# Expert products and channel moments on ScalarE, finer dealt preparation, and a spread ahead of the last stores, in a four-layer kernel

## The chip, the core and the metric

The kernel runs on one core of a Trainium2 chip. Its time is the device time of one execution in microseconds (us), and lower is better. A core has five engines that each execute their own instructions in order: TensorE (PE, with its weight loads shown as PEld), VectorE (DVE), ScalarE (ACT), GpSimd (POOL) and SyncE (SP, which in this kernel issues nearly all DMA transfers). They meet through semaphores. Tiles live in pools: a tile may be written only when those who used its place before are done.

## The reference, cut to what matters

Three images of 256 channels and 48 x 48 pixels go through four layers, each of the form x + layer(groupnorm(x)):

```python
x = x + conv1x1/attention block(_gn(x))          # layer 0
x = x + _L1_conv_ref(_gn(x), routing_ws, weight) # layer 1
x = x + _L2_conv_ref(_gn(x), weight, bias)       # layer 2
x = x + _L3_conv_ref(_gn(x), ...)                # layer 3, a scan over pixels

# layer 1: a 3x3 kernel of its own for each image
routing = sigmoid(pooled @ routing_ws)
ws = einsum('ne,eoihw->noihw', routing, weight)  # 8 experts
# layer 2: a 3x3 convolution with bias
# layer 3: (z, u projected; dt = softplus(...); causal conv of 4 taps)
hst = hst * exp(dt * A) + dt * B * u             # 512 rows x 16 states
y   = sum_n(hst * C) + u * D;  out = (y * silu(z)) @ out_proj
```

`_gn` is a group norm over 32 groups of 8 channels. Everything is float32.

## The kernel before, in words

An image is held in on-chip memory as `xs[b]`, 128 partitions x 2 channel halves x 2304 pixels. The images are handled in the order 2, 1, 0. Three parts follow one another.

**Layer 0** (to about 1600 us) has its order of instructions written out and pinned. Beside its end the kernel for image 2 of layer 1 is mixed.

**The conv stage** (about 1600 to 2140 us) does layers 1 and 2: six *units* (layer, image), two halves of an image each. Its order on each engine is chosen by a scheduler from the order of the program. A 3x3 convolution is done as six products per output block: `input_transform` pads and scales a half (ACT, L304, into `xpad`, of which there is one buffer), and twelve DVE instructions (L318 to L329) make `vt` of it (two buffers). `products` does six matmuls per product (L1331), `output` copies one of a pair (ACT, L1346, tile `cb`) and combines them on DVE (L1348 to L1361). Each half has two outputs of 128 channels; there are 144 matmuls in a unit. The product buffers in PSUM are five.

The kernels that are multiplied are made beside the units before. `mixed(b)` loads 48 pieces of 128 x 768, multiplies each by its image's routing weight and adds it up on DVE: L271 for expert 0, L273 for the other seven. `kernel_transform` (L254 to L259) follows. `plain` loads layer 2's kernel through a staging tile, copies it (L284) and transforms it. Unit 0 has `mixed(1)` beside it, unit 1 `mixed(0)`, unit 2 `plain`; each call of `next(beside...)` gives one step, 13 after each output. The transformed kernels `u` lie in two pools in turn.

Group norms of layers 2 and 3 are computed by `group_norm`: per image twelve `bn_stats` (DVE, L176) and two aggregations (L179), two small matmuls across the group (`ps_gm`, `ps_gv`), a few small DVE instructions, and a power on POOL (L162). The norm of layer 2 is called with the next unit's transform, that of layer 3 at the end of a unit of layer 2, where the image is also stored to memory (`xd`, L1401, six transfers on SP) so that the scan can fetch it in chunks.

From unit 4 on, `between()` in `output` deals one step of `early_preparation` at a time, four times in each output. These steps prepare chunk 0 of the scan and part of chunk 1: `group_scale` (ACT, L1043, with the image's norm), `less_mean` (PE, L1053), `centre`, `square_mean` (PE, L1060), `inverse_root`, `normalise`, `taps` (PE, L1095), `project_u` (L1115), `project_dt` (L1141), `softplus`. What is left is run when the units are done.

**The scan** (about 2140 us to the end) does layer 3 in 18 chunks of 384 pixels (6 per image), 8 steps each (four blocks of 128 rows, two halves of the states), order pinned again. `spread` fetches dt and dt*u of a block back from memory so that rows lie as the scan wants them: eight DMAs on SP, `dtr` (192 KB) and `dtur` (96 KB) in turn (L1444). In a step DVE fills half of a tile `hs` (L1474) and POOL the other half (L1478), ACT computes eight decays (L1503), DVE does eight scans (L1511; the first four on DVE's half, the last four on POOL's), POOL multiplies by C (`times_c`, L1519), and PE adds the states up (L1536). The program runs, ahead of step 0:

```python
k.rows = {0: spread(k, 0)}; spread_pe(k, 0); first_states(0); fill(0)
for n in range(3):
    decay(n)
for _, _, _, stage in gating:
    stage(k)
```

`gating` is the list of `project_z` (PE, L1172) and `take_z` (ACT, L1180) of a chunk; for later chunks these are dealt into the steps by `run`, with a last two of `take_z` in the list `after`.

Of the kernel before, what the change touches and what calls it, by code (L numbers as in the profile page):

```python
# [9 lines left out]
F32 = mybir.dt.float32  # L10
# [6 lines left out]
P = 128  # L17
B = 3
HW = 48
# [64 lines left out]
def net(  # L84
# [79 lines left out]

    def norm_steps(views, mat, psum, tag, stats=None):

# [3 lines left out]
        n = len(views)  # L170
        mv = small.tile([P, 2, 2], F32, name="mv")
        for i, view in enumerate(views):
# [32 lines left out]

    def group_norm_steps(b, psum, tag, stats=None):

        mv, gm, rstd = yield from norm_steps(
            [xs[b][:, ct, :] for ct in range(CT)], gmat, psum, tag, stats
        )  # L210
# [50 lines left out]
    def mixed(b, pool):  # L261

        u = weights[b] = pool.tile([P, 6, 3, CT, 256], F32, name="u")
        for e in range(EXPERTS):
            for ct in range(CT):
                for dx in range(3):
# [3 lines left out]
                    if e == 0:  # L270
                        nc.vector.tensor_scalar(dst, wt, re, None, ALU.mult)  # L271
                    else:
# [921 lines left out]
    def store(k, mo):  # L1194
# [63 lines left out]
    def early_preparation():  # L1258
# [4 lines left out]
        k = chunks[0]  # L1263
        yield
        group_scale(k)
        yield
# [27 lines left out]
        silu(k.u)  # L1294
        yield

        while 1 not in norm3:
            yield
# [6 lines left out]
        for m in (0, 2):  # L1305
# [7 lines left out]
            yield  # L1313
        k = chunks[1]
        for stage in (group_scale, less_mean, centre, square_mean, inverse_root, normalise):
            stage(k)
            yield
        tokens(k)


    with ExitStack() as l1:
# [5 lines left out]
        def products(u, vt, m, i):  # L1327
            pc = ps.tile([P, 512], F32, tag="c", name="ps_c")
            for ct in range(CT):
                for dy in range(3):  # L1330
# [3 lines left out]
                        start=ct == 0 and dy == 0, stop=ct == CT - 1 and dy == 2,  # L1334
                    )
            return pc[:, :HN]

        def output(b, h, m, u, vt, bias):
# [4 lines left out]
            for i, j in ((1, 3), (4, 5)):  # L1343
# [7 lines left out]
                sums += [add, sub]  # L1351
                between()
            p, q, r, s = sums
# [6 lines left out]
            for i, k, f in ((0, 0, 1.5), (2, 3, 6.0)):  # L1360
                stt(xj[:, k], products(u, vt, m, i), f, xj[:, k], ALU.mult, ALU.add)  # L1361
                between()

# [3 lines left out]
        halves = [(k, h) for k in range(len(units)) for h in range(2)]  # L1367

        def transformed(n):
            k, h = halves[n]  # L1370
            layer, b = units[k]
            if layer and h == 0:
                _, sc, sh = group_norm(b, pss, "s")
                norms[b] = sixth(sc, sh)
            return input_transform(b, h, *norms[b])
# [8 lines left out]
        vt = first_v  # L1384
        for n, (k, h) in enumerate(halves):
            layer, b = units[k]
# [11 lines left out]
            if layer and h == 1:  # L1398
                phases = xs[b].rearrange("p t (j n) -> p (t j) n", j=4)
                for c in range(NCH):  # L1400
                    nc.sync.dma_start(  # L1401
                        xd[b][:, c].rearrange("p t (j n) -> p (t j) n", j=4),
                        phases[:, :, c * (CH // 4) : (c + 1) * (CH // 4)],
                    )
                _, sc, sh = group_norm(b, pss, "s")
                keep = const.tile([P, 2, CT], F32, name=f"norm3{b}")
                nc.vector.tensor_copy(keep[:, 0, :], sc)
                nc.vector.tensor_copy(keep[:, 1, :], sh)
                norm3[b] = keep[:, 0, :], keep[:, 1, :]
        for _ in early:  # L1410
# [8 lines left out]
    with ExitStack() as l3:  # L1419
        wp = l3.enter_context(tc.tile_pool(name="w3", bufs=1))  # L1420
        psd = l3.enter_context(tc.tile_pool(name="psd", bufs=1, space=PSUM))
        psr = l3.enter_context(tc.tile_pool(name="psr", bufs=1, space=PSUM))
        psy = l3.enter_context(tc.tile_pool(name="psy", bufs=1, space=PSUM))

        scn = l3.enter_context(tc.tile_pool(name="scn", bufs=2))
        for name in ("u", "dtu", "bc0", "bc1", "sz"):
# [9 lines left out]
        def spread(k, m):  # L1436

            dtr = scn.tile([P, 4, CH], F32, name="dtr")
            dtur = scn.tile([P, 2, CH], F32, name="dtur")
            for i in range(4):  # L1440
                r = slice(32 * i, 32 * i + 32)
                for t, src in ((dtr, k.dtd), (dtur, k.dtud)):
                    src = src[m & 2][:, m & 1, :]
                    nc.sync.dma_start(t[r], src.rearrange("(q d) n -> d q n", d=32))  # L1444
# [267 lines left out]
```

## Time and profile before

| what | value |
|---|---|
| median of 3 runs | 3651.91 us |
| lowest, highest | 3649.39, 3655.53 us |
| the profiled execution | 3652.18 us, span 3650.2 us, granted clock 0.928 |
| busy PE, DVE, ACT, POOL | 3195.5, 3058.1, 2272.8, 1440.6 us |
| layer 0, conv stage, scan | about 1600, 540 and 1510 us |

The page and the views give times from the start of the span. A timeline row is: start, length (both us), engine, line, operation, out<-in with shapes, count, and in square brackets the idle time ahead of it and what ended that. A windows row is: start:end and length, then the busy time and number of instructions of PE, PEld, DVE, ACT and POOL, the granted clock of PE (1.00 is full), the mean busy share of the 16 DMA engines, and GB/s. One matmul of 128 x 128 by 128 x 288 shows as two records.

### The profile page before, as it was taken

How to read it: one execution, taken by the hardware profiler on the slowest of the kernel's cores; microseconds unless marked ns; L12 is line 12 of the kernel's file. 1: busy time of each engine (PE TensorE's matmuls, PEld its weight loads, DVE VectorE, ACT ScalarE, POOL GpSimd, SP SyncE). 2: the span in 40 equal slices, each digit the busy share in tenths (PEclk: the TensorE clock that was granted, in tenths of full speed). 3: DMA queues.
4: the chain of work that ended last, by engine and by line, in shares of the span. 5: the costliest groups of instructions: out<-in, count | busy, mean ns of one | idle time of the engine just before them, and what ended most of it. 6: DMA issues, size and time to landing. Idle time of an engine off the chain costs nothing. (4 is left out here: it accounts for less than half of the span.)

```text
span 3650.2 us, 45624 instructions
## 1 busy us (share of the span) xinstructions
PE 3195.5 (88%) x17154; PEld 1440.2 (39%) x17154; DVE 3058.1 (84%) x3398; ACT 2272.8 (62%) x3408; POOL 1440.6 (39%) x386
## 2 busy tenths in 40 slices
PE   6999999999999998877799987878888888878885
PEld 4323232342322324445577753333333333333331
DVE  3798989859889895479987559999999999999997
ACT  2688787748878874220012237777777777777774
POOL 0000000000000000210000039999999999999998
PEclk9999999999999999888899988988888999988887
DMA  4000000000000002645502223444444434443441
GB/s 172 10 1 1 1 2 1 1 39 1 1 1 1 1 1 79 209 140 208 203 19 65 51 72 99 102 117 103 114 108 105 107 97 110 101 119 99 115 105 36
DMA packets 167672, 266.50 MB, mean 73 GB/s; under 512 B 42689, under 2 KB 133633, under 8 KB 165266
## 3 DMA queue, kind: packets, MB, share of 16 engines
q1 hardware_dynamic: 155346, 245.80, 24.1%
q10 hardware_dynamic: 12096, 17.70, 1.5%
q8 instruction: 136, 2.23, 0.3%
q14 instruction: 94, 0.77, 0.1%
HBM read 216.31 MB, written 46.89 MB: 72 GB/s over the span
## 5 line engine op out<-in xcount | busy, mean ns | idle before, releaser
L597 ACT ACTIVATE pt<-ps_s 128x1024 f32<-128x1024 f32 x972 | 938.9, 1022 | 237.6 <-PE ps_s L593 220.2
L1511 DVE TENSOR_TENSOR_SCAN hs<-ps_da,hs 128x385 f32<-128x385 f32 x1152 | 1012.7, 939 | 71.9 <-ACT ps_da L1503 56.6
L673 DVE TENSOR_TENSOR part<-part,pt 128x2048 f32<-128x2048 f32 x396 | 906.5, 2289 | 78.5 <-ACT pt L597 53.9
L1503 ACT ACTIVATE ps_da<-dtr,u 128x384 f32<-128x384 f32 x1152 | 657.8, 582 | 314.6 <-DVE hs L1511 289.0
L162 POOL TENSOR_TENSOR rstd<-ve,mhalf 128x2 f32<-128x2 f32 (+1 forms) x26 | 17.3, 668 | 1683.1 <-DVE ve L160 1683.1
L593 PE MATMUL ps_s<-q,kt 32*128 32x512 f32 (+1 forms) x4320 | 616.8, 595 | 2.3 <-DVE q L554 0.9
L606 PE MATMUL acc<-pt,vt 128*32 128x512 f32 (+1 forms) x4320 | 523.7, 563 | 8.1 <-DVE o L653 8.0
L1331 PE MATMUL ps_c<-vt,u 128*128 128x288 f32 x1728 | 432.4, 412 | 65.4 <-DVE u L259 39.6
L1519 POOL TENSOR_TENSOR hc<-hs,x 128x3072 f32<-128x3072 f32 x72 | 444.4, 6172 | 48.6 <-PE ps_g L1141 15.6
L1519 POOL TENSOR_TENSOR hc<-hs,bc 128x3072 f32<-128x3072 f32 x72 | 444.0, 6167 | 36.2 <-PE ps_g L1141 13.6
L1331 PEld LDWEIGHTS ps_c<-vt,u 128*128 128x128 f32 x1728 | 331.4, 193 | 160.9 <-issue 67.3
L1095 PE MATMUL ps_g<-u 128*128 128x384 f32 x1152 | 385.9, 490 | 0.0
L593 PEld LDWEIGHTS ps_s<-q,kt 32*128 32x128 f32 x4320 | 219.9, 183 | 390.1 <-issue 230.2
L1095 PEld LDWEIGHTS ps_g<-u 128*128 128x128 f32 x1152 | 213.9, 189 | 170.2 <-issue 11.2
L1536 PE MATMUL ps_y<-hc,u 128*32 128x384 f32 x2304 | 244.1, 547 | 27.2 <-POOL hc L1519 23.9
L1478 POOL TENSOR_TENSOR hs<-dtur,x 128x1536 f32<-128x1536 f32 x72 | 247.8, 3442 | 19.4 <-DMA dtr<-dtd 11.5
L1478 POOL TENSOR_TENSOR hs<-dtur,bc 128x1536 f32<-128x1536 f32 x72 | 248.2, 3447 | 8.1 <-ACT ps_g L1073 4.9
L606 PEld LDWEIGHTS acc<-pt,vt 128*32 128x32 f32 x4320 | 95.7, 108 | 364.6 <-issue 329.0
L1346 ACT COPY cb<-ps_c 128x288 f32<-128x288 f32 x48 | 19.1, 398 | 297.6 <-PE ps_c L1331 248.8
L1141 PE MATMUL ps_g<-wconv,u 17*128 17x384 f32 x144 | 79.2, 684 | 97.2 <-ACT x L1162 97.2
L1172 PE MATMUL ps_g<-u 128*128 128x384 f32 x288 | 112.7, 526 | 39.1 <-ACT x L1180 23.3
L1053 PE MATMUL ps_g<-wconv,u 128*128 128x384 f32 x144 | 87.9, 784 | 67.3 <-ACT x L1162 67.3
(231 smaller groups left out, 3486.2 us busy)
## 6 DMA issues: line engine op xcount, KB each, us to landing
wconv<-in_we SPq DMA_DIRECT2D x144, 384.0 KB, 4.4
dtr<-dtd SPq DMA_DIRECT2D x288, 192.0 KB, 3.7
dtur<-dtud SPq DMA_DIRECT2D x288, 96.0 KB, 3.2
wconv<-xd SPq DMA_DIRECT2D x36, 384.0 KB, 4.4
x<-bcd SPq DMA_DIRECT2D x72, 192.0 KB, 5.7
dtd<-x SPq DMA_DIRECT2D x36, 384.0 KB, 2.4
bc<-bcd SPq DMA_DIRECT2D x72, 192.0 KB, 5.2
yc<-ycat ACTq DMA_DIRECT2D x18, 576.0 KB, 5.6
```

The costliest lines, as they stand in the source:

```text
L593: nc.tensor.matmul(s[:, j, cols], kt[r, mt * P : (mt + 1) * P], q[r, :n], start=True, stop=True,)
L597: nc.scalar.activation(p[:, h0 : h0 + 2, :], s, AF.Exp)
L606: nc.tensor.matmul(acc[h * HD : (h + 1) * HD, :n], vt[:, mt, g * P + h * HD : g * P + (h + 1) * HD], p[:, h, cols], start=mt == 0, stop=mt ...
L673: nc.vector.tensor_tensor(part, first_p if group == 1 else part, p, ALU.add)
L1095: nc.tensor.matmul(bank[m % 2], w3v["wtap"][:, tap, ct, m * P : (m + 1) * P], k.xn[:, ct, tap : tap + CH], start=tap == 0 and ct == 0, sto ...
L1172: nc.tensor.matmul(bank[j], w("in", ct * 512 + m * P, P), k.xn[:, ct, DCONV - 1 :], start=ct == 0, stop=ct == CT - 1,)
L1331: nc.tensor.matmul(pc[:, :HN], u[:, i, dy, ct, m * P : (m + 1) * P], vt[:, i, ct, dy * TW : dy * TW + HN], start=ct == 0 and dy == 0, stop ...
L1478: nc.gpsimd.tensor_tensor(hs[:, :, 2:4, 1:], k.rows[m][1].unsqueeze(1).broadcast_to([P, 2, 2, CH]), bb, ALU.mult,)
L1503: nc.scalar.activation(slots[n % 3][:, 1 : CH + 1], chunks[at].rows[m][0][:, q, :], AF.Exp, scale=amat[:, col : col + 1],)
L1511: nc.vector.tensor_tensor_scan(b, slots[(8 * s + part) % 3][:, : CH + 1], b, 0.0, ALU.mult, ALU.add)
L1519: nc.gpsimd.tensor_tensor(hc, tiles[s][:, :, :, 1:], cb.broadcast_to([P, 2, 4, CH]), ALU.mult)
L1536: nc.tensor.matmul(k.y_ps[32 * q : 32 * q + 32, :CH], fold, hc[:, g, q, :], start=False, stop=h == 1 and g == 1,)
```

## The change

1. `mixed`: the product of expert 0 is done by ACT (an activation Copy with the routing weight as its scale) rather than by DVE.
2. `plain`: layer 2's kernel is loaded straight into `u`, without staging tile and copy.
3. The norms of layers 2 and 3, all but the last image's, take their channel mean and variance from `moments`: on ACT, two passes per channel half over 2304 pixels, whose element output goes to a buffer of `xpad` that nobody reads. The rest of a norm (`next_norm`) is dealt out by `between()`.
4. `between()` is called after each product, six times in each output. The early preparation waits for the norm of image 2, the steps for chunk 1 come ahead of the wait for the norm of image 1, and `project_z` and `take_z` of chunk 0 are its last steps; the scan's start no longer runs `gating`, and the two `take_z` in `after` are left out for chunk 0.
5. The last image's stores to `xd` are issued by ACT's queue rather than SP's. The scan's two pools are given `reuse_waits="tile"`: a tile in them waits for those who used its own place, not for all of the pools that lay there. `spread` issues all four `dtr` ahead of the four `dtur`.

```diff
     def mixed(b, pool):
...
                     if e == 0:
-                        nc.vector.tensor_scalar(dst, wt, re, None, ALU.mult)
+                        nc.scalar.activation(dst, wt, AF.Copy, scale=re)
...
     def plain(pool):
...
-                wt = part_of_kernel(w2, ct, dx)
-                nc.vector.tensor_copy(u[:, dx, :, ct, :], wt)
+                nc.sync.dma_start(
+                    u[:, dx, :, ct, :],
+                    w2[ct * P : (ct + 1) * P, dx * 768 : (dx + 1) * 768].rearrange(
+                        "p (y o) -> p y o", y=3
+                    ),
+                )
...
-        (0, MID, 0, lambda k: take_z(k, 2, 0)),
-        (0, MID, 0, lambda k: take_z(k, 3, 1)),
+        (0, MID, 0, lambda k: k.at and take_z(k, 2, 0)),
+        (0, MID, 0, lambda k: k.at and take_z(k, 3, 1)),
...
     def early_preparation():
...
+        while 2 not in norm3:
+            yield
         group_scale(k)
...
+        k = chunks[1]
+        for stage in (group_scale, less_mean, centre, square_mean, inverse_root, normalise):
+            stage(k)
+            yield
+        tokens(k)
+        yield
+
+        k = chunks[0]
         while 1 not in norm3:
             yield
...
-        k = chunks[1]
-        for stage in (group_scale, less_mean, centre, square_mean, inverse_root, normalise):
-            stage(k)
+        for m in (0, 2):
+            for j in range(2):
+                project_z(k, m + j, j)
             yield
-        tokens(k)
+            for j in range(2):
+                take_z(k, m + j, j)
+            yield
...
         def products(u, vt, m, i):
...
+            between()
             return pc[:, :HN]
...
+        def moments(b):
+
+            mv = small.tile([P, 2, 2], F32, name="mv")
+            less = small.tile([P, CT], F32, name="lessm")
+            waste = pad.tile([P, 4, CT * (HR + 2) * PW + 2], F32, name="xpad")
+            waste = waste.rearrange("p j n -> p (j n)")[:, :N]
+            for ct in range(CT):
+                nc.scalar.activation(
+                    waste, xs[b][:, ct, :], AF.Identity, scale=1.0 / N,
+                    accum_out=mv[:, ct, 0:1],
+                )
+                nc.scalar.activation(
+                    less[:, ct : ct + 1], mv[:, ct, 0:1], AF.Identity, scale=-1.0 / HW
+                )
+                nc.scalar.activation(
+                    waste, xs[b][:, ct, :], AF.Square, bias=less[:, ct : ct + 1],
+                    scale=1.0 / HW, accum_out=mv[:, ct, 1:2],
+                )
+            return mv
+
+        def next_norm(layer, b):
+
+            last = layer and b == ORDER[-1]
+            known = None if last else moments(b)
+            for _ in range(5):
+                yield
+            _, sc, sh = yield from group_norm_steps(b, pss, "s", known=known)
...
         def between():
+            next(pending, None)
             if at_unit >= 4:
                 next(early, None)
...
+                queue = nc.sync if k + 1 < len(units) else nc.scalar
                 for c in range(NCH):
-                    nc.sync.dma_start(
+                    queue.dma_start(
...
+            if h == 1:
+                for _ in pending:
+                    pass
+                pending = next_norm(layer, b)
+                next(pending)
...
-        wp = l3.enter_context(tc.tile_pool(name="w3", bufs=1))
+        wp = l3.enter_context(tc.tile_pool(name="w3", bufs=1, reuse_waits="tile"))
...
-        scn = l3.enter_context(tc.tile_pool(name="scn", bufs=2))
+        scn = l3.enter_context(tc.tile_pool(name="scn", bufs=2, reuse_waits="tile"))
...
-            for i in range(4):
-                r = slice(32 * i, 32 * i + 32)
-                for t, src in ((dtr, k.dtd), (dtur, k.dtud)):
-                    src = src[m & 2][:, m & 1, :]
+            for t, src in ((dtr, k.dtd), (dtur, k.dtud)):
+                src = src[m & 2][:, m & 1, :]
+                for i in range(4):
+                    r = slice(32 * i, 32 * i + 32)
                     nc.sync.dma_start(t[r], src.rearrange("(q d) n -> d q n", d=32))
...
         for n in range(3):
             decay(n)
-        for _, _, _, stage in gating:
-            stage(k)
-
```

More of the change, by code (lines that the diff above doesn't have):

```diff
@@ L163, in rsqrt_eps, with norm_steps @@
         return r[:, :n]
-    def norm_steps(views, mat, psum, tag, stats=None):
+    def norm_steps(views, mat, psum, tag, stats=None, known=None):
         n = len(views)
-        mv = small.tile([P, 2, 2], F32, name="mv")
-        for i, view in enumerate(views):
+        mv = known
+        if known is None:
+            mv = small.tile([P, 2, 2], F32, name="mv")
+        for i, view in enumerate(views if known is None else ()):
             if stats is None:
@@ L204, in norm_stats, with group_norm_steps @@
         return at_once(norm_steps(*args))
-    def group_norm_steps(b, psum, tag, stats=None):
+    def group_norm_steps(b, psum, tag, stats=None, known=None):
         mv, gm, rstd = yield from norm_steps(
-            [xs[b][:, ct, :] for ct in range(CT)], gmat, psum, tag, stats
+            [xs[b][:, ct, :] for ct in range(CT)], gmat, psum, tag, stats, known
         )
@@ L1351, in output @@
                 sums += [add, sub]
-                between()
             p, q, r, s = sums
@@ L1361, in output @@
                 stt(xj[:, k], products(u, vt, m, i), f, xj[:, k], ALU.mult, ALU.add)
-                between()
         units = [(layer, b) for layer in range(2) for b in ORDER]
@@ L1367, in net @@
         halves = [(k, h) for k in range(len(units)) for h in range(2)]
+        def moments(b):
+            mv = small.tile([P, 2, 2], F32, name="mv")
+            less = small.tile([P, CT], F32, name="lessm")
[20 more added lines that the diff above has]
+            _, sc, sh = yield from group_norm_steps(b, pss, "s", known=known)
+            if layer == 0:
+                norms[b] = sixth(sc, sh)
+            else:
+                keep = const.tile([P, 2, CT], F32, name=f"norm3{b}")
+                nc.vector.tensor_copy(keep[:, 0, :], sc)
+                nc.vector.tensor_copy(keep[:, 1, :], sh)
+                norm3[b] = keep[:, 0, :], keep[:, 1, :]
         def transformed(n):
             k, h = halves[n]
[L1371 to L1375, printed above, removed]
+            return input_transform(units[k][1], h, *norms[units[k][1]])
         early = early_preparation()
@@ L1384, in net @@
         vt = first_v
+        pending = iter(())
         for n, (k, h) in enumerate(halves):
@@ L1404, in net @@
                     )
[L1405 to L1409, printed above, removed]
+            if h == 1:
[3 more added lines that the diff above has]
+                next(pending)
+        for _ in pending:
+            pass
         for _ in early:
```

## The prediction

> **What bounds the kernel now.** I read the rows in forty slices first, then windows over the conv stage, its waits, and the timeline around the seam to the scan. PE is full until slice 16, less so in slices 17 to 20, full again, and from slice 24 on POOL is. The change touches only the stretch from about 1600 us (first conv unit) to about 2180 us (second scan step). Windows over it (start:end, length, busy time and count of PE, PEld, DVE, ACT, POOL, granted clock, DMA share, GB/s):
>
> ```profile
> 1645.00:1700.00 55.00, 54.11 (x223) 41.76 (x221) 54.31 (x80) 5.07 (x8) 0.69 (x3) 1.00 0.68 236
> 1700.00:1725.00 25.00, 0.12 (x1) 0.15 (x1) 24.66 (x37) 0.00 (x0) 0.00 (x0) 0.60 0.57 206
> 1725.00:1797.00 72.00, 71.98 (x288) 55.76 (x288) 71.03 (x109) 8.33 (x12) 1.40 (x6) 0.97 0.62 210
> 1797.00:1819.00 22.00, 0.25 (x1) 0.28 (x2) 22.00 (x33) 0.00 (x0) 0.00 (x0) 0.58 0.45 155
> 1890.00:1966.00 76.00, 76.00 (x317) 59.67 (x316) 51.14 (x118) 8.69 (x13) 2.19 (x8) 1.00 0.13 39
> 2044.00:2139.00 95.00, 95.00 (x383) 71.30 (x381) 48.38 (x116) 21.80 (x34) 1.18 (x1) 1.00 0.25 63
> ```
>
> DVE is full up to 1819 while PE has two holes; afterwards PE is full and DVE half idle. So up to 1818.75, where PE starts unit 2, a microsecond off DVE is a microsecond; from there to the last conv matmul at 2139.24 (called E) only PE's work and stalls count. PE's timeline names what ended the holes:
>
> ```profile
> 1724.88 72.11 PE L1331 MATMUL ps_c<-vt,u 128*128 128x288 f32 x288 [24.98 <-issue]
> 1818.75 11.60 PE L1331 MATMUL ps_c<-vt,u 128*128 128x288 f32 x35 [21.77 <-DVE u L259]
> ```
>
> The second waits for DVE's last kernel transform, and so by DVE's full row does the first. Between 1818.75 and E PE waits once, 1.17 us at 1861.34 for a norm (mv L179). The products that the change moves:
>
> ```profile
> 1645.48 1.93 DVE L271 TENSOR_SCALAR u<-wconv,route 128x768 f32<-128x768 f32 x2
> 1647.68 3.77 DVE L271 TENSOR_SCALAR u<-wconv,route 128x768 f32<-128x768 f32 x4
> 1737.16 3.76 DVE L271 TENSOR_SCALAR u<-wconv,route 128x768 f32<-128x768 f32 x4
> 1743.42 1.92 DVE L271 TENSOR_SCALAR u<-wconv,route 128x768 f32<-128x768 f32 x2
> ```
>
> Both groups of six lie in the DVE-bound part; L176 (norm statistics, 35.8 us in this stage, all after 1833 us) and L284 (copies, from 1831 us) lie in the PE-bound one. The seam:
>
> ```profile
> 2140.09 2.83 SPq L1401 DMA_DIRECT2D xd<-x  x3
> 2147.53 1.76 DVE L1474 TENSOR_TENSOR hs<-ps_r,x 128x1536 f32<-128x1536 f32 x1 [2.99 <-DMA xd<-x]
> 2147.62 0.32 SPq L1444 DMA_DIRECT2D dtr<-dtd  x1
> 2154.90 1.59 ACT L1503 ACTIVATE ps_da<-dtr,u 128x384 f32<-128x384 f32 x3 [7.02 <-DMA dtr<-dtd]
> 2155.57 6.81 POOL L1478 TENSOR_TENSOR hs<-dtur,x 128x1536 f32<-128x1536 f32 x2 [11.51 <-DMA dtr<-dtd]
> 2160.92 1.81 DVE L1511 TENSOR_TENSOR_SCAN hs<-ps_da,hs 128x385 f32<-128x385 f32 x2 [2.74 <-ACT ps_da L1503]
> 2163.42 0.48 ACT L1180 COPY x<-ps_g 128x384 f32<-128x384 f32 x1 [2.03 <-PE ps_g L1172]
> 2166.97 2.66 DVE L1511 TENSOR_TENSOR_SCAN hs<-ps_da,hs 128x385 f32<-128x385 f32 x3 [4.25 <-ACT ps_da L1503]
> ```
>
> Here nothing is full: the spread (dtr, dtur) starts only when the last stores of x have landed, then the scans wait for decays (L1503), which stand behind take_z (L1180) on ACT, which waits for projections on PE. Step 0 ends at 2169.55, E + 30.3. Later POOL does 3.44 + 6.17 = 9.6 us in a pace of about 10.3 per step.
>
> **Part 1, first expert product on ACT.** Removed from DVE's full part: twice six at a pace of 0.93 us (3.76 for four), 11.2 us. The six for image 2 lie beside attention, where DVE isn't the limit: nothing. Two costs. The sixth product of unit 0 stands behind the wait for a staging buffer and before the second copy of a product (cb, L1346); the DMA that supplies L273 cost 2.0 us of waits in all before, and I take 0.7 more (0 to 3). And unit 1 now holds nine small instructions of unit 0's norm (rows of 0.13 to 0.17 us, 0.07 to 0.1 apart) that ran after 1860 before: 0.8. Net -9.7, range -7 to -12. The Trainium skill ("ScalarE: Activation LUTs", Rules for kernel authors) speaks against the move: multiplication belongs on VectorE. Its cost section on the same page makes one product 186 + 93 + 0.833 x 768 = 919 ns, an estimate. The rows: a 128x768 ACTIVATE took 844 ns (L1068), L271 took 1003 ns, and ACT was busy 5.07 of 55 us. If ACT were the limit, the rule would make this part nought; being idle it gives the 11.2. I go by the rows.
>
> **Part 2, copies and norms.** Kernel 2 is loaded straight into u: six copies less on DVE, 6 x 0.94 = 5.6 us. Five of six norms go to ACT: sixty L176 at 0.47 pace, 28 us. All that is cover removed from an engine that was half idle beside a full PE: 0, except that the 1.17 us stall goes. Had PE not been the limit there, it would be worth up to 34 us. The kernel's six loads wait for unit 1's last matmul; I place them about 20 us ahead of the first use. ACT gets, per unit, two Identity and two Square of 128x2304. From 128x768 (0.844) and 128x1536 (1.483), 0.833 us per 1000 elements, one takes an estimated 2.1 us, so 9 us per unit. They write to the padding buffer, of which there is one: the next unit's padding (L304) and transform wait. Counted from a unit's start S: norms to S+5, padding to S+8, twelve transform instructions at 0.72 to S+17; PE needs the result at S+35. Slack some 18 us: 0.
>
> **Part 3, finer dealing, and gates.** Preparation is dealt after each of six products per output instead of four times, and projections of z for chunk 0 (eight matmuls, 16 records of 0.34 at L1172) come into the full PE: +5.5. In the order of instructions as built, less_mean of chunk 0 stands 57 matmuls into unit 4, and now waits for group_scale on ACT, which waits for the norm of that image. Norm ready at S+27.7, two L1043 to S+30; PE is there at S+28: 2.0, and square_mean right behind it 0.6. Stage: -1.2 + 5.5 + 2.6 = +6.9, range +4 (no stall) to +12 (three more such stalls). No record of before shows this dealing.
>
> **Part 4, the seam.** Stores of the last image go to ACT's queue; the pools of the scan are released tile by tile, so the first dtr waits for E and not for the landing at about E+8; all dtr are issued ahead of dtur; take_z has left the start. Decays: four dtr issued E to E+1.9, landing 4.1 later by the row, E+6. DVE's first fill waits only for the norm chain, E+5.3 to E+7.1, so scans begin near E+7 (before E+16.3). POOL needs dtur. By the waits as built, the second to fourth dtur reuse the completion semaphores of the three last stores, so they are issued only when those have landed: stores issued by ACT at E+0.9 to E+2.8, landing 5.5 to 6.2 after issue, E+8.4; dtur lands 3.2 to 3.7 after that, E+12; POOL's 3.44 ends at E+15.5. DVE does four scans of its own half to E+10.6, waits, and four of POOL's at 0.9 by E+19.4. Before E+30.3, so -10.9. Of this the old stalls, 2.74 + 4.25 = 7.0, are take_z's. Range -8 to -15.3 (semaphores don't bind; then scans run without pause to about E+15). A new table load (1.28 us) is done before decay data arrive. The skill's page "DMA: Bandwidth & Descriptors" (Issuing engines are not separate DMA queues) says that another issuing engine saves only issue time: by that the store's move is worth at most 2.8 us, the row's issue time. The row of dtr at 2147.62 shows a wait for landing, 4.5 us past the last issue, and that wait is removed by the pools' release, not by the queue; so the rule bounds one edit, and I keep 10.9.
>
> **Part 5, steady scan.** Same instructions in the same order on PE, DVE, ACT and POOL. Within a spread dtr comes first, the last dtur is still eighth. 0, but 0.1 us per spread over 72 would be 7 us, so I allow 5 either way.
>
> **Sum.** -9.7 + 6.9 - 10.9 = -13.7 on the profiled run of 3652.18 (span 3650.2 and 2.0 around it), 0.3 above the median 3651.91: 3638.5, about -0.37 %. This kernel's measurement can tell about 0.2 % from no change, 7.3 us.
>
> **Rivals.** (a) The semaphores of the stores don't hold up dtur, and the dealing makes no stall: -9.7 + 4.3 - 15.3 = -20.7, 3631. For: dtur waits are for single transfers, which may land sooner with less traffic. Against: the waits are in the program. Chance 0.2. (b) Gains are given back: two or three more dealing stalls (+5), 7 instead of 9.7 and 8 instead of 10.9: -3.1, 3649, within 0.2 %. For: DVE and ACT execute in order, and one late preparation step delays the copies and sums that free PE's product buffers. Against: units 4 and 5 had no stall before at a coarser dealing. Chance 0.12. (c) Slower: the hand-overs PE to ACT to DVE to PE in units 4 and 5. With six dealings per output they are one product apart, 12 records of 0.243, 2.9 us, not 4.4. A step that takes copy 0.48, table loads of 1.28 and two ACTIVATEs of 0.84 is longer than 2.9, and PE then stands still. Some twelve hand-overs; the sum turns at 13.7 / 12 = 1.1 us each, and 2 us each gives 3651.9 - 13.7 + 24 = about 3662. Against: I find only the two stalls of part 3. Chance 0.04. (d) The change doesn't do what it says: the spread isn't ahead of the last stores, since dtur waits for them; that is half in my forecast already. If dtr also waited, scans would start at E+16 as before and only take_z's 7.0 be won: -9.8, 3642. Chance 0.14. My forecast: 0.5.
>
> **How the numbers follow.** Cases (a), (d), the forecast and none of (b) and (c) are faster by over 0.2 %, apart from the forecast's own tail: 0.84; within 0.2 % 0.12; slower 0.04. Extremes of the bounds are -12 + 4 - 15.3 = -23 and -7 + 12 - 8 = -3; with the scan's 5 allowed in part, I take 3625 to 3648.
>
> **What would show it.** Right: DVE's full stretch shorter by about 10 with holes of PE near 20 and 17 us; unit 2 start to E about 327; a stall at L1053 in unit 4 near 2 us; first scan about E+7, a wait of DVE for POOL after four scans, step 0 done at E+19; dtur issued in a gap after the landing of xd. Wrong: E later than about 2139 (stalls in units 4, 5, or padding late in units 2 to 5), scans running through without a pause (rival a), or a pace per scan step different from before.

## The result, and the profile after

The changed kernel takes 3634.6 us (median of 4, 3633.98 to 3637.25) against 3653.21 for the kernel before in the same measurement (median of 4): ratio 0.9951, interval [0.9934, 0.9969]. Its profiled run is 3635.14 us with a span of 3633.4, 16.8 less than before's 3650.2. Run once more beside other kernels it took 3635.49, ratio 0.9962 [0.9949, 0.9976]. The kernel before varies by 13.4 us (3642.25 to 3655.68 over all its later runs); in that second measurement it took 3647.02, so the gain is 11.5 us there and 18.6 in the first. Sizes below therefore come from stretches of single profiles, each between two events that every kernel has. Lines of code have moved: L1331 is L1348, L271 is L273, L1444 is L1497, L1503 is L1556, L1511 is L1564, L1478 is L1531, L1180 is L1186.

| stretch | before | after | after, a second profile | predicted difference | measured, first profile |
|---|---|---|---|---|---|
| start to first conv matmul | 1625.3 | 1627.8 | 1627.8 | 0 | +2.5 |
| first conv matmul to start of unit 2 | 193.5 | 183.0 | 182.2 | -9.7 | -10.5 |
| unit 2 to the last conv matmul (E) | 320.5 | 325.0 | 323.7 | +6.9 | +4.5 |
| E to the end of step 0 | 30.3 | 18.2 | 18.2 | -10.9 | -12.1 |
| from there to the end of the span | 1480.7 | 1479.5 | 1481.8 | 0 | -1.2 |
| sum | | | | -13.7 | -16.8 |

The windows of after, with the edges put where its holes are:

```profile
1645.00:1701.00 56.00, 56.00 (x234) 43.69 (x232) 55.94 (x92) 7.19 (x12) 0.00 (x0) 1.00 0.64 223
1701.00:1720.70 19.70, 0.92 (x4) 0.51 (x3) 19.70 (x27) 13.01 (x13) 0.69 (x3) 0.58 0.73 246
1720.70:1793.00 72.30, 72.23 (x290) 56.09 (x290) 70.47 (x123) 10.38 (x15) 2.09 (x4) 0.97 0.59 202
1793.00:1810.70 17.70, 0.59 (x2) 0.50 (x2) 17.70 (x22) 7.40 (x7) 0.69 (x3) 0.59 0.62 201
1880.00:1966.00 86.00, 86.00 (x358) 67.46 (x357) 47.70 (x107) 25.83 (x32) 2.87 (x11) 1.00 0.21 60
2044.00:2135.80 91.80, 91.76 (x366) 68.05 (x364) 44.94 (x106) 29.13 (x42) 1.38 (x4) 1.00 0.27 65
```

The third busy time in a row is DVE's. DVE is still full through both holes of PE, which are 19.7 and 17.7 us long instead of 25 and 22. DVE is still the limit there, only with less to do. ACT's busy time in the first hole went from 0 to 13.01 us: products and norms lie there now. In the dense part PE stays full and DVE has still less to do.

PE's timeline of after. The first two rows end the holes; the third is the only stall of the dense stretch; the last two are the projections of z that have come in:

```profile
1720.72 22.54 PE L1348 MATMUL ps_c<-vt,u 128*128 128x288 f32 x84 [14.20 <-issue]
1810.72 23.62 PE L1348 MATMUL ps_c<-vt,u 128*128 128x288 f32 x84 [12.29 <-DVE u L261]
1982.94 3.05 PE L1059 MATMUL ps_g<-wconv,u 128*128 128x384 f32 x8 [0.33 <-ACT wconv L1049]
2112.97 2.75 PE L1178 MATMUL ps_g<-u 128*128 128x384 f32 x8
2121.38 2.75 PE L1178 MATMUL ps_g<-u 128*128 128x384 f32 x8
```

The seam of after, E at 2135.76 (SPq and ACTq are the engines' DMA queues):

```profile
2135.84 1.81 SPq L1497 DMA_DIRECT2D dtr<-dtd  x4
2136.29 3.66 ACTq L1452 DMA_DIRECT2D xd<-x  x3
2137.74 7.35 SPq L1497 DMA_DIRECT2D dtur<-dtud  x4
2143.18 1.28 ACT L1556 ACT_TABLE_LOAD   x1 [2.99 <-DMA dtr<-dtd]
2145.10 3.51 DVE L1564 TENSOR_TENSOR_SCAN hs<-ps_da,hs 128x385 f32<-128x385 f32 x4 [2.62 <-ACT ps_da L1556]
2147.06 6.80 POOL L1531 TENSOR_TENSOR hs<-dtur,x 128x1536 f32<-128x1536 f32 x2 [6.82 <-DMA dtur<-dtud]
2150.52 3.51 DVE L1564 TENSOR_TENSOR_SCAN hs<-ps_da,hs 128x385 f32<-128x385 f32 x4 [1.91 <-POOL hs L1531]
2153.94 1.73 DVE L1527 TENSOR_TENSOR hs<-ps_r,x 128x1536 f32<-128x1536 f32 x1
```

dt is issued at E, not 8 us later. The four dtur issues are drawn out over 7.35 us; SP's waits name the landing of xd for three of them (5.4 us in all). By the trace's landing times the second and third store landed at E + 7.59 and 9.02, and the third and fourth dtur were issued at E + 7.61 and 9.03. DVE does four scans, pauses for POOL's half, and does four more, as forecast. No take_z stands between the decays.

### The profile page after: what moved, and what is told of

Its sections match the earlier page's. It is cut to its first block, busy times and chain, and to the rows that moved or that the text cites. A ratio compares the mean times of both kernels' runs of the same rounds, so it can differ in the third digit from the quotient of the medians.

```text
span 3633.4 us, 45544 instructions
## 1 busy us (share of the span) xinstructions
PE 3195.8 (88%) x17154; PEld 1441.3 (40%) x17154; DVE 3007.2 (83%) x3304; ACT 2338.1 (64%) x3477; POOL 1442.2 (40%) x386
## 5 line engine op out<-in xcount | busy, mean ns | idle before, releaser
L1564 DVE TENSOR_TENSOR_SCAN hs<-ps_da,hs 128x385 f32<-128x385 f32 x1152 | 1012.7, 939 | 61.1 <-ACT ps_da L1556 43.2
L1556 ACT ACTIVATE ps_da<-dtr,u 128x384 f32<-128x384 f32 x1152 | 658.2, 582 | 311.0 <-DVE hs L1564 292.6
L1348 PE MATMUL ps_c<-vt,u 128*128 128x288 f32 x1728 | 432.1, 412 | 44.4 <-DVE u L261 30.2
L1572 POOL TENSOR_TENSOR hc<-hs,x 128x3072 f32<-128x3072 f32 x72 | 445.9, 6193 | 36.7 <-PE ps_g L1147 13.4
L1572 POOL TENSOR_TENSOR hc<-hs,bc 128x3072 f32<-128x3072 f32 x72 | 443.8, 6165 | 37.2 <-PE ps_g L1147 13.6
L1101 PE MATMUL ps_g<-u 128*128 128x384 f32 x1152 | 388.3, 492 | 3.1 <-ACT u L1110 3.1
L1348 PEld LDWEIGHTS ps_c<-vt,u 128*128 128x128 f32 x1728 | 331.6, 193 | 139.5 <-issue 33.4
L1531 POOL TENSOR_TENSOR hs<-dtur,x 128x1536 f32<-128x1536 f32 x72 | 248.3, 3449 | 16.2 <-DMA dtur<-dtud 12.8
L1531 POOL TENSOR_TENSOR hs<-dtur,bc 128x1536 f32<-128x1536 f32 x72 | 248.2, 3447 | 6.9 <-DMA dtur<-dtud 4.3
L1364 ACT COPY cb<-ps_c 128x288 f32<-128x288 f32 x48 | 19.1, 397 | 221.6 <-PE ps_c L1348 203.4
L1589 PEld LDWEIGHTS ps_y<-hc,u 128*32 128x32 f32 x2304 | 64.6, 118 | 200.5 <-issue 148.0
```

The costliest lines, as they stand in the source:

```text
L1101: nc.tensor.matmul(bank[m % 2], w3v["wtap"][:, tap, ct, m * P : (m + 1) * P], k.xn[:, ct, tap : tap + CH], start=tap == 0 and ct == 0, sto ...
L1348: nc.tensor.matmul(pc[:, :HN], u[:, i, dy, ct, m * P : (m + 1) * P], vt[:, i, ct, dy * TW : dy * TW + HN], start=ct == 0 and dy == 0, stop ...
L1531: nc.gpsimd.tensor_tensor(hs[:, :, 2:4, 1:], k.rows[m][1].unsqueeze(1).broadcast_to([P, 2, 2, CH]), bb, ALU.mult,)
L1556: nc.scalar.activation(slots[n % 3][:, 1 : CH + 1], chunks[at].rows[m][0][:, q, :], AF.Exp, scale=amat[:, col : col + 1],)
L1564: nc.vector.tensor_tensor_scan(b, slots[(8 * s + part) % 3][:, : CH + 1], b, 0.0, ALU.mult, ALU.add)
L1572: nc.gpsimd.tensor_tensor(hc, tiles[s][:, :, :, 1:], cb.broadcast_to([P, 2, 4, CH]), ALU.mult)
```

## Experiments

All are the changed kernel with one edit, but for the run of one part alone. "Stretch to unit 2" starts at the first conv matmul; "seam" is E to the end of step 0. The changed kernel has 183.0, 325.0 (dense stretch) and 18.2.

### Products back on DVE

```diff
-                        nc.scalar.activation(dst, wt, AF.Copy, scale=re)
+                        nc.vector.tensor_scalar(dst, wt, re, None, ALU.mult)
```

> The changed kernel with one part undone: the product of expert 0 is back on DVE. My theory: DVE is the limit from the first unit to the start of unit 2, so that stretch (first conv matmul to the first one of unit 2, 183.0 us in the changed kernel, 193.5 before) grows by twice 5.6, to 193 to 195, both holes of PE by about 5, and the rest of the kernel stays: about 3645 us. Rival: the shorter stretch comes from the norms that left DVE, and the products only moved a wait for their data to ACT: then the stretch stays within 2 us of 183 and the time near 3635.

3645.02 us (21 runs), ratio to before 0.9986 [0.9979, 0.9993]. Stretch to unit 2: 195.9, 12.9 more than in the changed kernel; dense stretch 323.8, seam 18.3. PE's timeline of this run, at the second hole:

```profile
1804.05 0.59 PE L184 MATMUL ps_gm<-mv,gmat 128*128 128x2 f32 x2 [8.98 <-ACT xpad L1392]
1819.22 3.25 PE L1348 MATMUL ps_c<-vt,u 128*128 128x288 f32 x6 [14.59 <-DVE u L261]
```

8.98 + 14.59 us of idle where the changed kernel has 4.89 + 12.29. The rival (the norms made the stretch shorter) falls. The stretch is 2.4 us longer than before's 193.5: the rest of the change costs something there; what, was not traced.

### One part alone: the products, on the kernel before

The same line the other way round, in the kernel before.

> The kernel before with one part alone: expert 0's product by ACT for all three images. My theory: the stretch from the first conv matmul to unit 2 goes from 193.5 to about 181 (12 to 13 us shorter, as the undoing showed), the first conv matmul is 2 to 3 us later, the dense stretch (320.5) and the seam (30.3) stay: about 10 us faster than before. Rival: the relief of DVE needs the other parts (the norms out of its way), then less than 5 us.

3637.89 us, ratio 0.9974 [0.9964, 0.9985]. Stretch to unit 2: 181.5, 12.0 less than before; dense stretch 320.6, seam 29.4. PE's timeline of this run, with idle of 20.37 and 16.01 us where before has 24.98 and 21.77:

```profile
1722.25 71.52 PE L1331 MATMUL ps_c<-vt,u 128*128 128x288 f32 x288 [20.37 <-issue]
1809.78 20.48 PE L1331 MATMUL ps_c<-vt,u 128*128 128x288 f32 x75 [16.01 <-DVE u L259]
```

This one line carries the gain of the stretch, and the rival (that the norms must first be out of DVE's way) falls. 12.0 is the twelve instructions at 0.93 (11.2) and the 0.78 us stall of before at 1685.08, which is gone from this trace; that this stall makes the difference is read off, not tested. The first conv matmul came at 1628.3, 3 us later than in before's profile; see the last experiment.

### Statistics back on DVE

```diff
-            known = None if last else moments(b)
+            known = None
```

> The changed kernel with the channel statistics of all norms back on DVE (twelve statistics instructions per image, not the passes on ACT), dealt at the same places. Sixty instructions at 0.47 us, 28 us, go back to DVE. My theory: those of units 2 to 5 lie beside a full PE and cost nothing; but the statistics of unit 0's and unit 1's image now start right at the end of their unit, where DVE is the limit, so up to 24 x 0.47 = 11 us may show in the stretch to unit 2 if the scheduler puts them ahead of products, and none if it puts them behind. From unit 2's start to the last conv matmul: 325 us, unchanged within 1. Time 3635 to 3646. Rival (relief of DVE counts everywhere): more than 20 us slower, with the dense stretch longer than 330.

3642.51 us, ratio 0.9978 [0.9968, 0.9987]. Stretch to unit 2: 190.0, 7.1 more; dense stretch 325.3, seam 18.0. The group of statistics in the window from 1640 us to unit 2 of this run:

```profile
L178 DVE BATCH_NORM_STATS2 bnst<-x 128x6 f32<-128x384 f32 x12 | 5.7, 537 | 0.0
```

So one image's twelve fell into DVE's full part, 5.7 of the 7.1 us (the other 1.4 were not traced); the other norms lie beside the full PE and cost nothing: 0.2 us in the dense stretch for the other 48 instructions. In the kernel before all of them lay beside the full PE, so the move of statistics to ACT should gain nothing there; that was not run. It pays because the change also starts the norms earlier, where DVE is full.

### Gates back at the start, behind the decays

```diff
-        for m in (0, 2):
-            for j in range(2):
-                project_z(k, m + j, j)
-            yield
-            for j in range(2):
-                take_z(k, m + j, j)
-            yield
...
         for n in range(3):
             decay(n)
+        for _, _, _, stage in gating:
+            stage(k)
```

(The two take_z in `after` are back too.)

> The changed kernel with the projections and copies of z of chunk 0 back at the scan's start, behind the first decays, as before. My theory: 16 matmul records at 0.34 leave the dense stretch (325.0 to 319.5), and ACT's copies of z stand between the decays again, so step 0 ends 4 to 7 us later after the last conv matmul than the 18.1 of the changed kernel: net between -1 and +2 us against the changed kernel, 3634 to 3637. Rival: the copies of z hide under the wait for dt*u, then the start stays at 18 and the kernel gains 5.5, about 3629.

3635.93 us, ratio 0.9959 [0.9945, 0.9973]. Dense stretch 319.8 (5.2 less), seam 24.2 (6.0 more). From its seam:

```profile
2146.05 0.48 ACT L1186 COPY x<-ps_g 128x384 f32<-128x384 f32 x1 [3.02 <-PE ps_g L1178]
2147.05 0.96 DVE L1556 TENSOR_TENSOR_SCAN hs<-ps_da,hs 128x385 f32<-128x385 f32 x1 [2.74 <-ACT ps_da L1548]
2153.10 2.66 DVE L1556 TENSOR_TENSOR_SCAN hs<-ps_da,hs 128x385 f32<-128x385 f32 x3 [3.91 <-ACT ps_da L1548]
```

The stalls of before are back, 2.74 and 3.91 us: ACT executes the copies in order ahead of decays, and each copy waits for PE. Putting z into the full PE wins 6.0 at the seam and pays 5.2 for it, so this part of the change is close to nothing in sum.

### Gates at the start, ahead of the decays

```diff
+        project_z(k, 0, 0)
+        project_z(k, 1, 1)
+        take_z(k, 0, 0)
+        take_z(k, 1, 1)
+        project_z(k, 2, 0)
+        project_z(k, 3, 1)
         for n in range(3):
             decay(n)
```

(z out of early_preparation as above; the last two copies come within step 0, by the list `after`.)

> As the run before, but the projections of z use both banks and their first two copies stand ahead of the first decays on ACT, where it waits for dt anyway; the last two copies come within step 0, where DVE waits for POOL's half. My theory: the dense stretch gives back 5.5 us (319.5), and step 0 still ends about 18 us after the last conv matmul, since POOL's half, which waits for dt*u, sets it: about 3629 us, faster than the changed kernel by 5. Rival: the copies wait for PE at a halved clock and push the decays back, step 0 ends at 22 or later and nothing is gained.

3630.33 us, ratio 0.9946 [0.9932, 0.9959]; 4.3 below the changed kernel's median. Dense stretch 318.3, seam 19.6. The two copies stand where ACT waits for dt anyway. The dense stretch is 6.7 us shorter, of which 1.5 is chance (PE's clock at its start, below), and 1.4 are lost at the seam: the stores landed 8.1 to 8.7 us after their issue here (6.6 to 7.4 in the changed kernel), and POOL's half waits for them. Why they took longer was not settled.

### The seam, one edit at a time

Stores on SP's queue:

```diff
-                queue = nc.sync if k + 1 < len(units) else nc.scalar
+                queue = nc.sync
```

> The changed kernel with the last image's stores back on SP's queue, ahead of the spread. My theory: issue order costs at most the three issues (2.8 us), dt lands that much later, but dt*u waits for the landing of the stores as before, and POOL's half, which waits for it, sets the end of step 0: 18 to 19.5 us after the last conv matmul against 18.2, kernel within 1.5 us of the changed one. Rival: the move to ACT's queue is what puts the spread ahead of the stores; without it, dt waits for the landing and step 0 ends at 22 or later.

3636.06 us; seam 19.5 (+1.3). dt lands later: the table load ahead of the first decay comes at E + 10.7 instead of E + 7.4. The rival (dt waits for the landing) falls. The size came as expected, but not quite for the expected reason: the scans begin at E + 12.6 and all eight run without a pause, so DVE no longer waits for POOL's half, and dt sets the end.

Pools released as a whole:

```diff
-        wp = l3.enter_context(tc.tile_pool(name="w3", bufs=1, reuse_waits="tile"))
+        wp = l3.enter_context(tc.tile_pool(name="w3", bufs=1))
...
-        scn = l3.enter_context(tc.tile_pool(name="scn", bufs=2, reuse_waits="tile"))
+        scn = l3.enter_context(tc.tile_pool(name="scn", bufs=2))
```

> The changed kernel without the tile-by-tile release of the scan's two pools. My theory: the first dt transfer waits for the landing of the last stores, 7 to 8 us after the last conv matmul, so decays start near 14 and step 0 ends at 22 to 24 instead of 18.2: 4 to 6 us slower than the changed kernel. Rival: the waits of the transfers for the stores' semaphores already cover this, then nothing changes (18 to 19).

3637.46 us; seam 21.1 (+2.9), E at 2135.42. Its spread:

```profile
2142.03 1.75 SPq L1497 DMA_DIRECT2D dtr<-dtd  x4
2143.82 1.84 SPq L1497 DMA_DIRECT2D dtur<-dtud  x4
```

It starts at E + 6.6, but then dtur follows without a pause, since the stores have landed (4.5 us after issue by the median). The eight scans run without a pause from E + 14.1, so here too dt sets the end and not POOL's half. That makes it less than I expected (4 to 6): what dt loses, the pause of DVE gives back in part.

dt and dt*u in turn:

```diff
-            for t, src in ((dtr, k.dtd), (dtur, k.dtud)):
-                src = src[m & 2][:, m & 1, :]
-                for i in range(4):
+            for i in range(4):
+                for t, src in ((dtr, k.dtd), (dtur, k.dtud)):
+                    src = src[m & 2][:, m & 1, :]
                     r = slice(32 * i, 32 * i + 32)
```

> The changed kernel with dt and dt*u transfers in turn, as before. My theory: the transfers that reuse the stores' semaphores are now the sixth to eighth, of which two are of dt*u and one of dt; the last dt part is issued after the stores have landed, so the decays start near 12 instead of 8.7 us after the last conv matmul, and DVE's first four scans end about when POOL's half is there: step 0 ends at 19 to 21 instead of 18.2, +1 to +3 us. Later spreads: no change in pace. Rival (the order in the steady scan matters, 72 spreads): 5 us or more, spread over the scan.

3633.57 us; seam 18.9 (+0.7). From its seam, E at 2132.20:

```profile
2144.28 6.91 DVE L1564 TENSOR_TENSOR_SCAN hs<-ps_da,hs 128x385 f32<-128x385 f32 x8 [5.36 <-ACT ps_da L1556]
```

As expected the last dt is held up: the table load comes at E + 10.2 and the first scan at E + 12.1. POOL's half starts at E + 11.0, about as in the changed kernel, and is done before DVE's own four scans are, so the eight run without a pause and dt ends last. The order within a spread is worth little here, and no more in the steady scan: from the end of step 0 the run takes 1480.5 us, within the 1478.8 to 1481.8 of all profiles with the change or parts of it.

Stores issued by POOL:

```diff
-                queue = nc.sync if k + 1 < len(units) else nc.scalar
+                queue = nc.sync if k + 1 < len(units) else nc.gpsimd
```

> The changed kernel with the last image's stores issued by POOL, whose transfers use other semaphores than those of SP and ACT. My theory (the shared semaphores hold back dt*u): dt*u is issued right behind dt and lands near 8.5 us instead of 11.3, POOL's half ends near 12 instead of 14.7, step 0 ends near 15 to 16: 2 to 3 us faster than the changed kernel. Rival (traffic): the DMA engines are busy from 4 to 12 us after the last conv matmul at over 300 GB/s, dt*u lands at 11 anyway, and step 0 ends at 18. A third: POOL's issues delay the norm and its half, step 0 later than 19.

3632.84 us, ratio 0.9952 [0.9936, 0.9969]; seam 16.7 (-1.5). The spread of this run (E at 2134.41):

```profile
2136.34 3.30 SPq L1497 DMA_DIRECT2D dtur<-dtud  x4
2144.24 6.81 POOL L1531 TENSOR_TENSOR hs<-dtur,x 128x1536 f32<-128x1536 f32 x2 [5.16 <-DMA dtur<-dtud]
```

dtur is issued within 3.3 us instead of 7.35, and POOL's half, which waits for it, starts at E + 9.8, against 11.3. So both theories hold a part: the wait for the stores costs 1.5 us, and the rest fits the traffic, stores and spread of 1.15 MB each moving at once; that part is read from the rates below, not tested. The transfers of the changed kernel from 2130 to 2150, forty slices of 0.5 us (busy tenths of the DMA engines, GB/s):

```profile
DMA  0000000000000479899999999999640467999999
GB/s 0 0 0 0 0 0 0 0 0 0 0 0 0 80 178 246 267 288 314 313 336 274 327 357 321 332 311 284 151 144 0 120 151 252 338 187 224 237 215 191
```

From 2138 to 2144 the 16 engines are over 80 % busy, at 267 to 357 GB/s.

### Layer 0, and the changed kernel again

> The changed kernel itself once more, beside the other three of this call on the same chip: 3634.6 within 2 us, and the stretches as in its first profile (first conv matmul at 1626 to 1629, 183.0 us to unit 2, 325.0 to the last conv matmul, 18.2 to the end of step 0).

3635.49 us. First conv matmul at 1627.8, then 182.2, 323.7 and 18.2. The dense stretch is 323.5 to 323.8 or 325.0 to 325.3 in all profiles of kernels with z in it. The difference lies in the first matmuls of unit 2, where PE comes out of its hole at half clock. The windows of the first profile of the changed kernel (unit 2 starts at 1810.72) and of the second (1810.05); the last but two is the granted clock:

```profile
1813.60:1816.60 3.00, 3.00 (x7) 2.05 (x7) 3.00 (x5) 0.00 (x0) 0.00 (x0) 0.50 0.00 0
```

```profile
1813.60:1816.60 3.00, 3.00 (x14) 2.37 (x13) 3.00 (x5) 0.00 (x0) 0.00 (x0) 1.00 0.00 0
```

The half clock ends at 1816.8 in the first and at 1813.4 in the second. In the profiles of 325.0 to 325.3 us (and 319.8 without z) it lasts 5.8 to 6.1 us into unit 2, in those of 323.5 to 323.8 (and 318.3 to 318.5 without z) 2.9 to 3.4, so 1.3 to 1.5 us of the stretch is no difference between kernels. The kernel before has 5.8 and compares with the long ones.

Image 2's product back on DVE:

```diff
-                    if e == 0:
+                    if e == 0 and b == ORDER[0]:
+                        nc.vector.tensor_scalar(dst, wt, re, None, ALU.mult)
+                    elif e == 0:
                         nc.scalar.activation(dst, wt, AF.Copy, scale=re)
```

> The changed kernel with expert 0's product of image 2 alone back on DVE (it lies beside the end of layer 0); images 1 and 0 stay on ACT. My theory now: the six products in ACT's pinned order there shift PE's waits so that PE's clock stays at half for 10 us instead of 4 near 1550 us; without them the first conv matmul comes at 1623 to 1626 instead of 1626 to 1629, the stretches after it are unchanged (183, 325, 18), and the kernel is 2 to 3 us faster than the changed one. Rival: the later start is chance, then the half-clock stretch is 10 us long here too and the time is the same.

3632.02 us (3627.69 to 3636.25), ratio 0.9958 [0.9945, 0.9972]: 3.5 below the changed kernel by medians, but with a spread of 8.6. In its profile the first conv matmul comes at 1619.9. The 2.5 us between the first profiles of before and after arise in one place. PE's timeline before, and after:

```profile
1551.99 0.91 PE L479 MATMUL ps_s<-cur,wf 128*128 128x384 f32 x2 [0.73 <-ACT f L483]
```

```profile
1551.79 1.65 PE L485 MATMUL ps_s<-cur,wf 128*128 128x384 f32 x2 [0.73 <-ACT f L489]
```

The same matmuls take nearly twice as long. The window over this place, before and after:

```profile
1551.50:1557.00 5.50, 4.28 (x14) 2.47 (x15) 2.66 (x7) 1.86 (x4) 0.00 (x0) 1.00 0.54 203
```

```profile
1551.50:1557.00 5.50, 5.21 (x10) 2.95 (x10) 0.90 (x4) 0.81 (x2) 0.00 (x0) 0.50 0.32 125
```

The half clock lasts from 1548.1 to 1551.5 before and from 1547.1 to 1557.4 after, beside the same idle of 5.2 us: 3.4 us and 10.2. All ten profiles with image 2's product on ACT have the long stretch at half clock; of four with it on DVE, three have the short one (before, the first experiment, this one). The fourth is the last experiment, whose row at 1546.36 has 1.65 us again.

So DVE there does not prevent it, and the theory of the expectation, that ACT's products cause it, is not shown. Nor is this place all of the difference: the run's first conv matmul comes 7.9 us ahead of the changed kernel's. Two earlier places vary in the same way, one near 1420 us, where the half clock lasts 6.8 to 13.7 us in the 14 profiles, and one near 1480, where it lasts 3.4 us in this run and the last and 10.2 in the other twelve (a pair of matmuls took 0.91 us at 1481.97 here and 1.65 at 1484.48 before). All 14 profiles together have the first conv matmul between 1619.9 and 1628.8. The Trainium skill ("TensorE: Matmul & The Clock Gate", Part 1) has the clock decided on windows of 3.4 us that run free of the kernel; the lengths seen, 3.4, 6.8, 10.2 and 13.7 us, are one to four of these, and which of them a program meets would depend on the phase. What sets the phase here stays open.

### A version that beats both

z at the start ahead of the decays, the last stores by POOL, image 2's product on DVE.

> Three edits on the changed kernel together: z of chunk 0 at the scan's start ahead of the decays, last stores issued by POOL, image 2's product on DVE. If they add up: 4.3 (z) and 1.5 to 2.5 (stores) and 2.5 (layer 0) faster than the changed kernel, about 3626. Dense stretch 318 to 320, step 0 ends 16.5 to 18 after the last conv matmul, first conv matmul at 1623 to 1626. Rival: the copies of z wait behind a slow PE when dt comes earlier, and only one of the first two gains shows: 3628 to 3630.

3623.72 us (3622.06 to 3625.81), ratio to before 0.9932 [0.9919, 0.9946], 11.8 below the changed kernel on the same chip (3635.49). Dense stretch 318.5, seam 17.3, first conv matmul at 1622.4. Of the 13.6 us between this profile's span and that of the changed kernel's second one (3633.8), 5.5 lie ahead of the first conv matmul, 5.2 in the dense stretch, 0.9 at the seam, and some 2 in the scan behind it. The edits of z and stores add up about as they should; the part ahead of the conv stage comes mostly from the two earlier places of half clock, and whether the edit of image 2's product has a hand in it is open, as is the part in the scan.

## Why the prediction was right, and where not

The direction and the places were right, and so were the mechanisms of the two large terms, the products and the seam. That the sum came so near (16.8 in the profiles, 13.7 forecast) is in part luck: the three stretches that the forecast is about gave -18.1 in the first profile and -20.2 in the second, and layer 0's +2.5, which it had not foreseen, took some of that back. Term by term:

- **Products (forecast -11.2 + 0.7 for supply).** Measured -12.0 alone, -12.9 by undoing. The 0.7 of supply was not needed: ACT's products waited 12.4 us for data in seven waits, and the profile names nobody who waited for them. The rule against multiplying on ACT, which the prediction cites, would have kept this part at nought; it is worth as much as the whole seam. The page's reason is speed in bf16, and here, in float32, a product took 934 ns on ACT and 1003 on DVE. The duration came nearer to the page's estimate (919) than to my row of an ACTIVATE without a scale operand (844).
- **Small instructions of the norm in DVE's full part (+0.8).** About right: the changed kernel's stretch is 1.5 and 0.7 us longer in its two profiles (183.0, 182.2) than with the products alone (181.5). The undoing of the products left it 2.4 longer than before; the difference was not traced.
- **Copies and norms off DVE (0, cover).** Right for the norms as they lay before; the run with statistics on DVE adds what I had not written: with the earlier start of the norms 7.1 us are at stake. The copies of layer 2's kernel and the finer dealing were not tried alone.
- **Dealing (+2.6 of stalls).** Right place, wrong size: the stall is at less_mean in unit 4, 0.33 us, and none at square_mean. With 288 records to a unit, unit 4 starts near 1954.3; the norm was ready 27.5 us later (1981.8), as forecast (27.7), and PE was there at 28.3. The step that failed is that PE waits for both group_scale instructions: its first matmul needs only the first of them, and it started before the second had ended (1982.94 against 1981.80 + 1.94).
- **z in the full PE (+5.5).** Two rows of 2.75 us: exact; taking it out again shortened the stretch by 5.2. Its return at the seam (7.0 forecast) is 6.0.
- **Seam (-10.9).** Measured -12.1. Both halves of my reasoning held, dt*u behind the stores' landing and POOL's half as the last to end. POOL's half started at E + 11.3 (12 forecast) and ended near 14.7 (15.5), step 0 at 18.2 (19.4, where the sum of 15.5 and four scans of 0.9 is 19.1). The first scan came at E + 9.3 and not 7.1, for two reasons. The last dt landed 5.9 us after its issue, with the stores moving beside it, against 4.1 forecast and 4.1 in the run with pools released as a whole, where they had landed; and the table load, forecast as done by then, stood behind the wait for dt (2143.18, 1.28 us). That cost nothing, because POOL's half ends last. But the slack is small: with pools, queue or order undone dt sets the end, so these three do not add up. By single undoing: gates 6.0, pools 2.9, store queue 1.3, order 0.7. The store queue's 1.3 is within the 2.8 that the rule on issuing engines, cited in the prediction, allows.
- **Layer 0 (0).** The step "nothing" for image 2 was off by 2.5 us in the profile, from the half clock, whose length I had not put into the range.
- **Steady scan (0).** Right: -1.2 up to the end in the first profile and +1.1 in the second, with 1478.8 to 1481.8 over all profiles with the change or parts of it.

Rival (a), no stall and unhindered dtur, came half true: the stall was nearly absent, the seam gained 12.1 of its 15.3. The semaphores did hold up dtur.

## What to carry to other kernels

Take work off the engine that is full in that stretch, also onto an engine that needs longer for it (an image's statistics took ACT some 10 us and DVE 5.7), if that engine is idle there; ask of each moved instruction where it will lie, not only which engine it leaves (statistics cost nothing in one place and 7 us in another). At a seam, list what each first instruction waits for and find the last to arrive: here the gates' copies in ACT's order were worth 6 us, and they could be had without paying for them in the full stretch, by standing where their engine waited anyway. Compare stretches between common events, not only totals, when the runs vary by nearly as much as the change.

## What the runs showed of the hardware

- After the same 5.2 us of idle PE ran at half clock for 3.4 us before and for 10.2 us in the changed kernel, the longer costing 2.5 us. At the places looked at, the half clock lasted 3.4 us or a multiple of it in all 14 profiles (3.4 to 27.3 us).
- Stores of 384 KB landed 7.0 us after issue (median) with a spread issued ahead of them by another queue, and 8.4 in another run of that order. With nothing else moving they took 4.5 us in one run and 5.9 in the kernel before, and 4.6 with the spread behind them on the same queue. So traffic fits, but does not explain all of it.
- In one and the same kernel PE's half clock reached 6.1 us into a stretch of full work in one profile and 3.4 in another, and the stretch was 1.3 us longer in the first.
- A pass over 128x2304 with an accumulated sum took 2.13 us on ACT (2.22 with a bias operand), and reading the sum a further 0.19 us.
